# A long-convolution tail on one core: the last half source gets a program and loads of its own

## The chip, the cores and the metric

The kernel runs on one core of a Trainium2 chip. The metric is device time in microseconds (us) for one execution, the lower the better. TensorE (PE) does the matrix products, VectorE (DVE), ScalarE (ACT) and GpSimd (POOL) do elementwise work, and SyncE (SP) issues every DMA transfer of this kernel, strictly in the order of the program. All data are 32-bit floats.

## The reference

Two layers work on an image batch of shape (4, 128, 64, 64), that is 4 sequences of 4096 tokens with 128 channels. Layer 0 (a convolution gate, a sort of patches and a small state-space scan) doesn't matter here. Layer 1 adds two parts to the tokens: a state-space scan over 256 state entries (`_L1_attn_ref`), and a spectral convolution (`_L1_ffn_ref`) of the normalised sum. The second is what the change touches:

```python
Vf = jnp.fft.rfft(phi, n=n, axis=0)
Uf_p = jnp.fft.rfft(u, n=n, axis=1)
Uf_m = jnp.fft.rfft(u * sgn3, n=n, axis=1)          # sgn3: +1, -1, +1, ...
U_plus = jnp.fft.irfft(Vf[None, :, :, None] * Uf_p[:, :, None, :], n=n, axis=1)[:, :sl]
U_minus = jnp.fft.irfft(Vf[None, :, :, None] * Uf_m[:, :, None, :], n=n, axis=1)[:, :sl]
U_minus = U_minus * sgn[None, :, None, None]
...
out = jnp.einsum('btkd,k,kde->bte', U_plus, s, Mpp)
out = out + jnp.einsum('btkd,k,kde->bte', U_minus, s, Mpm)
```

It is a causal convolution of every channel with 16 filters (index k), once plain and once with alternating sign, each followed by a 128 x 128 matrix. A short convolution over three tokens (`_compute_ar_u`) is added, and four branches of decreasing length are mixed with weights. The output at a token depends on all tokens before it, so the last tokens' outputs can only be finished when the scan has ended.

## The kernel before

**Layer 1's main loop.** The program is written out by hand in its final order; no scheduler moves anything. `parts` lists 32 parts, each a chunk of 512 tokens of one sequence; the last one is chunk 7 of sequence 3. A part has 256 steps, one for each state entry. A step scans two rows of 512 tokens on DVE (`scan`, L1236) in place in `ring`, an SBUF tile of five slots; one slot holds four steps (VD = 4). POOL fills a slot (L1220), ACT makes the decay factors (L1232). Every eight steps (GD = 8, two slots) PE contracts the two slots with the matrix c (L1266), in six pieces of which one is taken at each of the following steps. ACT moves the result out of PSUM, a DMA puts it into DRAM (`yd`), and four small DMAs (L1292, "takes") read a skewed view of it back into the tile `yt`.

**The output of a part.** `output` (L979) turns `yt` of a finished part into tokens: it loads x2 (L984) and the gate (L986), transposes yt in two halves of 128 columns (L991), multiplies by the gate (L993), multiplies by W_out (L997), adds x2 (L999), transposes (L1005), normalises, reverses the tokens' order with a flip product (L1016) and copies them into a tile `tok` (L1018). Then it transposes once more (L1022), makes the three-token convolution (L1036) and writes the sum to DRAM as x3 (L1039). It is a generator: inside the loop `beside` runs it piece by piece at steps of the next part. It yields at the points where PE or another engine should take the next bit. PSUM has one bank for all these products (`middle`).

**The spectral program.** Tokens are kept apart by parity (even and odd), so a block of 1024 tokens is a tile of 2 parities x 4 groups of 128 tokens x 128 channels, reversed in time. A task names an output block, the source blocks whose tokens it takes, and whether it ends the block (`full`) or leaves a partial sum in DRAM. `products` (L1096) works tasks off as items, one for each output parity r, filter k and side (the parity of the taps). An item loads a strip of the filter, a window of up to 896 values that slides by one from partition to partition (L1093), and a matrix (L1087), three items ahead and into three strip buffers and four matrix buffers. It multiplies tok by the strip (L1179, the convolution), ACT copies the result out of PSUM (L1191), and a second product with the matrix (L1121) adds it to `fin`. At the end of an r, the partial sum is added by a product with the identity (L1129) and the result to x3 (L1137); after r = 1 a DMA stores the output block (L1139).

**The last block.** Block 3 of sequence 3 is made in stages. Its last stage takes the source's second half, the groups 2 and 3 of 128 tokens of each parity, which are the last part's tokens. It has 2 x 16 x 2 = 64 items; each has convolution products of 256 and 128 columns, an eviction of 256 columns and a second product of 256 columns. It comes after the loop: first the leftover pieces and takes, then the last output with spectral work between its pieces, then `go_on` (L1386) until the spectral program has been idle 16 times.

Of the kernel before, what the change touches and what calls it, by code (L numbers as in the profile page):

```python
# [8 lines left out]
F32 = mybir.dt.float32  # L9
AF = mybir.ActivationFunctionType  # L10
ALU = mybir.AluOpType
# [4 lines left out]
NB = 4  # L16
# [641 lines left out]
TS = 512  # L658
NCH = L // TS
NT = TS // 128  # L660
GD = 8
VD = 4
NQ = 5
NK = 16
# [241 lines left out]
def layer1(ctx: ExitStack, tc, ident, weights, work, psum, second, phi, pqd, mud, x, omd, permd, first, x2, x3, out):  # L906
# [15 lines left out]
    nc = tc.nc  # L922
# [3 lines left out]
    wk = ctx.enter_context(tc.tile_pool(name="s_wk", bufs=2))  # L926
    sp = ctx.enter_context(tc.tile_pool(name="s_sp", bufs=3))
# [3 lines left out]
    pc = ctx.enter_context(tc.tile_pool(name="s_pc", bufs=2, space=PSUM))  # L931
    pf = ctx.enter_context(tc.tile_pool(name="s_pf", bufs=1, space=PSUM))
# [4 lines left out]
    wo, at = weights[3:]  # L937
# [3 lines left out]
        out=flip, in_=flip, compare_op=ALU.not_equal, fill=1.0, base=-127, pattern=[[1, 128]],  # L941
# [35 lines left out]
    tokens = {}  # L977

    def output(b, ch, yt, gate):  # L979


        cols = bass.ts(ch, TS)
        xr = small()
        nc.sync.dma_start(xr, x2[b][:, cols])  # L984
        yk = wide()
        nc.sync.dma_start(yk, gate)  # L986
        for k in range(2):
            yield "mm"
            ps = middle()
            for i in range(NT):  # L990
                nc.tensor.transpose(ps[:, bass.ts(i, 128)], yt[:, i, bass.ts(k, 128)], ident)  # L991
            yield "post"
            nc.vector.tensor_tensor(yk[:, k, :], ps, yk[:, k, :], ALU.mult)  # L993
        yield "mm"
        ps = middle()
        for k in range(2):
            nc.tensor.matmul(ps, wo[:, k, :], yk[:, k, :], start=k == 0, stop=k == 1)  # L997
        yield "post"
        nc.vector.tensor_tensor(xr, xr, ps, ALU.add)  # L999
        yield "mm"  # L1000
        pair = xr.rearrange("p (a q) -> p q a", q=2)
        tp = middle()
        for r in range(2):
            for i in range(2):
                nc.tensor.transpose(tp[:, bass.ts(2 * r + i, 128)], pair[:, r, bass.ts(i, 128)], ident)  # L1005
        yield "post"
        tk = small()
        nc.scalar.copy(tk, tp)
        yield "free"
        yield from normalise(tk.rearrange("p (i c) -> p i c", i=NT))  # L1010
        yield "mm"
        if ch % 2 == 0:
            tokens[b, ch // 2] = sp.tile([128, 2, 4, 128], F32, tag="tok", name="tok", bufs=6)
        tok = tokens[b, ch // 2]
        ps = middle()
        nc.tensor.matmul(ps, flip, tk, start=True, stop=True)  # L1016
        yield "post"
        nc.scalar.copy(tok[:, :, bass.ts(ch % 2, 2), :], ps.rearrange("p (r i c) -> p r i c", r=2, i=2))  # L1018
        yield "mm"
        up = middle()  # L1020
        for i in range(NT):
            nc.tensor.transpose(up[:, bass.ts(i, 128)], tk[:, bass.ts(i, 128)], ident)  # L1022
        mu = small()[:, 0:384].rearrange("p (i c) -> p i c", i=3)
        nc.sync.dma_start(mu, mud[:, (0, 1, 2, 2, 3, 3, 3, 3)[ch]])
        yield "post"
        ut = sm.tile([128, 2 + TS], F32, tag="t2", name="ut", bufs=3)
        nc.scalar.copy(ut[:, 2:].rearrange("p (a q) -> p q a", q=2), up.rearrange("p (q a) -> p q a", q=2))
        if ch:
            nc.scalar.copy(ut[:, 0:2], halos[b % 2])
        else:  # L1030
            nc.scalar.activation(ut[:, 0:2], ident[:, 0:2], AF.Copy, scale=0.0)
        nc.scalar.copy(halos[b % 2], ut[:, TS:])
        yield "mm"
        ps = middle()
        for i in range(3):
            nc.tensor.matmul(ps, mu[:, i, :], ut[:, bass.ds(2 - i, TS)], start=i == 0, stop=i == 2)  # L1036
        yield "post"
        nc.vector.tensor_tensor(xr, xr, ps, ALU.add)
        nc.sync.dma_start(x3[b][:, cols], xr)  # L1039
        if (b, ch) == (NB - 1, NCH - 2):  # L1040
            add([(b, 3, [(3, range(2))], True, False)])
        elif (b, ch) == (NB - 1, NCH - 1):
            add([(b, 3, [(3, range(2, 4))], True, True)])
        elif ch % 2:
            block(b, ch // 2)

    later = []
    queue = []  # L1050
    strips, mats = {}, {}
    row = 128 + L // 2
    now = [0]
    partial = dr.tile([2, 4, 2, 128, TS], F32, name="partial", bufs=1)

    def block(b, blk):

        if b < NB - 2:  # L1060
            tasks = [(b, blk, range(blk + 1), False, True)]
        else:
            tasks = (
                [(b, 0, [0], False, True), (b, 2, [0], False, False), (b, 3, [0], False, False)],
                [(b, 1, [0, 1], False, True), (b, 2, [1], True, False), (b, 3, [1], True, False)],
                [(b, 2, [2], True, True), (b, 3, [2], True, False)],
                [(b, 3, [3], True, True)],
            )[blk]
        add([(b, blk, [(src, range(4)) for src in srcs], *rest) for b, blk, srcs, *rest in tasks])

    def add(tasks):
        for task in tasks:
            queue.extend(
                (task, r, k, side, n)
                for r in range(2) for k in range(NK) for side in range(2) for n in range(len(task[2]))
            )
# [132 lines left out]
    def carry(b, ch, d, ready):  # L1209

        af, vf = ready[4:]
        last = lasts[b % 2]
        cols = bass.ds(d, 128)
        if ch:
            nc.gpsimd.tensor_tensor(af[:, :, cols], af[:, :, cols], last[:, :, cols], ALU.mult)
            nc.gpsimd.tensor_tensor(vf[:, :, cols], vf[:, :, cols], af[:, :, cols], ALU.add)
# [88 lines left out]
    parts = [(b, ch) for b in range(NB - 2) for ch in range(NCH)]  # L1305
    parts += [(b, ch) for ch in range(NCH) for b in (NB - 2, NB - 1)]
    ready = {0: first}
    dls = {}
    ring = wk.tile([128, NQ, VD, 2, TS], F32, name="ring", bufs=1)
    steps = 256 * len(parts)  # L1310
    pieces = []
    side, kind = None, None
    spectral, credit = products(), 0

    def beside(n):

        if n:
            yield from output(*parts[n - 1], done.pop(n - 1), ready.pop(n - 1)[2])
        else:
            yield from put_back()  # L1320
        if n + 1 < len(parts):
            ready[n + 1] = tiles(n + 1)
            yield from project(*parts[n + 1], ready[n + 1])

    done, takes = {}, []
# [9 lines left out]

    for k in range(-12, steps):
        now[0] = k
        j = k + 10
        if 0 <= j < steps and j % 128 == 0:
            carry(*parts[j // 256], j % 256, ready[j // 256])  # L1340
        j = k + 6
        if 0 <= j < steps and j % VD == 0:
            spread(j // VD, j % 256, dls[j // VD], ready[j // 256])
        j = k + 1
        if 0 <= j < steps:
            lift(j % 256, factors[j % 2], dls[j // VD])
        j = k + 10
        if 0 <= j < steps and j % VD == 0:
            dls[j // VD] = fetch(j % 256, ready[j // 256])
        j = k + 2  # L1350
        if 0 <= j < steps and j % VD == 0:
            begin(j // VD, j % 256, ready[j // 256])
        if k < 0:
            continue
        due()
        n, d = divmod(k, 256)
        b, ch = parts[n]
        if pieces:
            pieces.pop(0)()
        scan(k, factors[k % 2])  # L1360
        if d % GD == GD - 1:
            more, take = contract((k - GD + 1) // VD, ready[n][1], d // GD, lasts[b % 2] if ch + 1 < NCH else None)
            pieces += more
            takes.append((n, take))
        if d == GD:
            side = beside(n)
            kind = next(side, None)
        at_step = d % GD
        if kind == "free" or (kind == "mm" and at_step == 6) or (kind == "post" and at_step == 7):
            kind = next(side, None)  # L1370
        if at_step == GD - 1:
            fetch_y(n, d)
        pace = 1.4 if n < 2 * NCH else 1.7
        credit = min(credit + pace * TS, pace * TS)
        while credit > 0:
            cost = next(spectral)
            if cost == 0:
                break
            credit -= cost
    for piece in pieces:  # L1380
        piece()
    while takes:
        fetch_y(len(parts), 0)
    idle = 0

    def go_on():  # L1386
        nonlocal idle
        now[0] += 1
        due()
        idle = 0 if next(spectral) else idle + 1  # L1390

    for _ in beside(len(parts)):
        go_on()
        go_on()
    idle = 0
    while idle < 16:
        go_on()


@with_exitstack  # L1400
# [72 lines left out]
```

## Time and profile before

| | |
|---|---|
| Median of 3 runs | 21174.41 us (21171.87 to 21175.32) |
| The profiled execution, its own time | 21175.71 us |
| Its span in the profile | 21174.0 us |
| Busy: PE, DVE, ACT, POOL | 17593.0, 20421.0, 15775.4, 19750.3 us |
| Mean granted PE clock | 0.917 |
| Last scan step ends | 21000.9 us |
| Tokens of the last part copied (L1018 starts) | 21032.32 us |
| First product of the last stage starts | 21045.46 us |
| Last add on DVE, and last store issued | 21169.58 and 21170.30 us |

Times in the tail count from the start of the span. The busy shares are of the whole span, of which the part after the last scan step is 173 us. A float product shows as two records in the profile, so "x4" are two products. A line number names the line of the kernel that issued an instruction, and "DMA a<-b" is a transfer's time until landing.

### The profile page before, as it was taken

The numbers are of one execution on the slowest core, as the hardware profiler recorded it, in microseconds if no ns is written. First come the engines' busy times: TensorE is split into PE (matmuls) and PEld (weight loads), VectorE is DVE, ScalarE is ACT, GpSimd is POOL, SyncE is SP. The second block draws the span as 40 slices with busy tenths as digits, with TensorE's granted clock in tenths as the row PEclk, the third lists the DMA queues.
The fourth block names the chain that finished last, engine by engine and source line by source line (L and its number), as shares of the span: only waits on it lengthen the run. The fifth ranks groups of instructions, "written<-read, shape, count | busy, mean of one in ns | idle before, by whom it ended". The sixth has DMA issues, their size and how long they took to land.

```text
span 21174.0 us, 282862 instructions
## 1 busy us (share of the span) xinstructions
PE 17593.0 (83%) x99308; PEld 7771.7 (37%) x99308; DVE 20421.0 (96%) x11805; ACT 15775.4 (75%) x28243; POOL 19750.3 (93%) x3541
## 2 busy tenths in 40 slices
PE   7788844655858888877768999599999999999997
PEld 4344421322323333333323344243434434344434
DVE  7799999999999999999999999999999999999996
ACT  3667667777777777777777777788887787788875
POOL 2666699999999999999999999999999999999996
PEclk8999966777979999988979999699999999999999
DMA  1555544555656666666656777577777777777776
GB/s 68 133 143 144 144 163 155 185 172 174 220 176 221 223 226 224 223 208 199 205 192 221 231 240 238 174 237 234 239 236 231 235 234 235 237 234 233 232 224 187
DMA packets 2204928, 4303.20 MB, mean 203 GB/s; under 512 B 770633, under 2 KB 1290097, under 8 KB 1938161
## 3 DMA queue, kind: packets, MB, share of 16 engines
q1 hardware_dynamic: 2203504, 4285.10, 63.0%
q8 instruction: 786, 12.88, 0.2%
q14 instruction: 638, 5.22, 0.1%
HBM read 3660.02 MB, written 624.17 MB: 202 GB/s over the span
## 4 chain that ended last, share of the span: by engine, by line
DVE 53%; issue 15%; PE 11%; ACT 4%; POOL 3%; DMA 1%; SPq 0%; DVEq 0%; POOLq 0%; ACTq 0%
DVE ring L1236 52%; PE conv L1179 6%; POOL ring L1220 3%; PE yp L1266 3%; ACT da L1232 2%; PE fin L1121 1%; DMA strip<-in_phi 1%; ACT conved L1191 1%; PE mm L1036 0%; PE mm L883 0%; PE mm L877 0%; PE mm L868 0%; ACT t L804 0%; ACT ye L1273 0%; DVE st L789 0%
## 5 line engine op out<-in xcount | busy, mean ns | idle before, releaser
L1220 POOL TENSOR_TENSOR ring<-u,dlb 128x4088 f32<-128x4088 f32 x2048 | 18074.9, 8892 | 70.5 <-DMA dlb<-delta 42.1
L1236 DVE TENSOR_TENSOR_SCAN ring<-da,ring 128x1024 f32<-128x1024 f32 x8192 | 17927.9, 2266 | 182.4 <-ACT da L1232 154.0
L1232 ACT ACTIVATE da<-dlb,at 128x511 f32<-128x511 f32 x16384 | 11321.1, 691 | 4052.2 <-DVE ring L1236 3766.3
L1179 PE MATMUL conv<-strip,tok 128*128 128x512 f32 (+3 forms) x20480 | 8632.2, 549 | 83.0 <-DMA strip<-in_phi 82.0
L1266 PE MATMUL yp<-ring,c 128*32 128x256 f32 x65536 | 4931.5, 430 | 2482.1 <-DVE ring L1236 1284.9
L1179 PEld LDWEIGHTS conv<-strip,tok 128*128 128x128 f32 x20480 | 3652.7, 191 | 4172.4 <-issue 3732.6
L1266 PEld LDWEIGHTS yp<-ring,c 128*32 128x32 f32 x65536 | 2011.7, 119 | 6185.4 <-issue 3454.8
L532 POOL TENSOR_TENSOR v<-dx,bcb 128x1024 f32<-128x1024 f32 x512 | 1208.6, 2361 | 631.7 <-DVE states L554 627.5
L1121 PE MATMUL fin<-conved,pq 128*128 128x512 f32 (+1 forms) x3968 | 1789.0, 543 | 9.1 <-ACT sum L1142 4.8
L546 ACT ACTIVATE f<-dt,an 128x255 f32<-128x255 f32 x2048 | 974.7, 476 | 490.9 <-DVE states L554 440.2
L554 DVE TENSOR_TENSOR_SCAN states<-f,v 128x1024 f32<-128x1024 f32 x512 | 1176.0, 2297 | 106.1 <-ACT f L546 54.5
L1273 ACT COPY ye<-yp 128x512 f32<-128x512 f32 x2048 | 1185.9, 579 | 24.1 <-PE yp L1266 23.1
L1191 ACT COPY conved<-conv 128x512 f32<-128x512 f32 (+1 forms) x1728 | 986.7, 571 | 255.4 <-PE conv L1179 252.4
L570 PE MATMUL y<-p,ident 128*128 128x512 f32 x2048 | 1010.4, 619 | 173.7 <-DVE p L558 170.1
L1121 PEld LDWEIGHTS fin<-conved,pq 128*128 128x128 f32 x3968 | 664.8, 192 | 387.1 <-issue 279.1
L558 DVE TENSOR_TENSOR p<-states,bcb 128x1024 f32<-128x1024 f32 x512 | 627.0, 1225 | 38.3 <-DVE states L554 0.4
L570 PEld LDWEIGHTS y<-p,ident 128*128 128x128 f32 x2048 | 364.6, 194 | 710.0 <-issue 336.6
L1226 ACT COPY ring<-vf 128x8 f32<-128x8 f32 x2048 | 386.8, 189 | 4.1 <-DMA omd<-om 4.1
L462 PE MATMUL mm<-ow,yg 128*32 128x128 f32 x2048 | 250.8, 276 | 39.0 <-ACT om L466 37.7
L462 PEld LDWEIGHTS mm<-ow,yg 128*32 128x32 f32 x2048 | 219.3, 133 | 136.2 <-ACT om L466 60.8
L1279 ACT COPY last<-ring 128x8 f32<-128x8 f32 x1792 | 267.0, 198 | 0.0
L407 PE MATMUL mm<-xin,taps 128*128 128x512 f32 x512 | 236.3, 605 | 22.8 <-ACT an L378 19.9
(229 smaller groups left out, 5356.2 us busy)
## 6 DMA issues: line engine op xcount, KB each, us to landing
dlb<-delta SPq DMA_DIRECT2D x2048, 1024.0 KB, 5.3
strip<-in_phi SPq DMA_DIRECT2D x1536, 448.0 KB, 5.0
yd<-ye SPq DMA_DIRECT2D x2048, 256.0 KB, 4.6
strip<-in_phi SPq DMA_DIRECT2D x1088, 256.0 KB, 4.8
bcb<-bcd SPq DMA_DIRECT2D x1024, 256.0 KB, 4.2
pq<-pqd SPq DMA_DIRECT2D x1472, 64.0 KB, 4.2
yt<-yd SPq DMA_DIRECT2D x4096, 4.0 KB, 4.4
pq<-pqd SPq DMA_DIRECT2D x256, 128.0 KB, 4.2
```

The source lines that it names most:

```text
L532: nc.gpsimd.tensor_tensor(v, ready[n][2][:, :, bass.ts(i, SUB)].unsqueeze(1).broadcast_to((128, 2, 2, SUB)), bc[:, 0].unsqueeze(2).broadca ...
L546: nc.scalar.activation(factors[j % 2][:, a, k, 1:], ready[n][1][:, k, SUB * i + 1 : SUB * i + SUB], AF.Exp, scale=an[:, k, 2 * g + a : 2 * ...
L554: nc.vector.tensor_tensor_scan(states.rearrange(flat), factors[j % 2].rearrange(flat), v.rearrange(flat), 0.0, ALU.mult, ALU.add)
L570: nc.tensor.matmul(t.rearrange("p k t -> p (k t)"), ident, p[:, a].rearrange("p k t -> p (k t)"), start=g == 0 and a == 0, stop=False, ski ...
L1121: nc.tensor.matmul(fin[:, bass.ds(c0, w)], pq[:, n, :], u[:, bass.ds(c0, w)], start=begin and n == 0, stop=end and not partly, skip_group_ ...
L1179: nc.tensor.matmul(ps[:, skip:], tok[:, 1 - r if side else r, j, :], strip[:, bass.ds(c0 - lo, TS - skip)], start=which == 0 and j == js[0 ...
L1191: nc.scalar.copy(u[:, cols], ps[:, cols])
L1220: nc.gpsimd.tensor_tensor(ring[:, q % NQ, :, :, 1:], ready[0][:, :, 1:].unsqueeze(1).broadcast_to((128, VD, 2, TS - 1)), dl[:, :, 1:].unsq ...
L1232: nc.scalar.activation(da[:, h, 1:], dl[:, d % VD, 1:], AF.Exp, scale=at[:, h, d : d + 1])
L1236: nc.vector.tensor_tensor_scan(v, da.rearrange("p h t -> p (h t)"), v, 0.0, ALU.mult, ALU.add)
L1266: nc.tensor.matmul(yp[i // 2][bass.ts(p, 32), i % 2], c[:, h, t], moving(h, 128 * i + 32 * p, 32), start=h == 0, stop=h == 1,)
L1273: nc.scalar.copy(ye, yp[j].rearrange("p i d t -> p i t d"))
```

## The change

The last stage no longer goes through `products`. A generator of its own, `last_products`, computes it for both output parities at once: for each filter k and token parity p it multiplies tok by a window with 256 columns for each of the two output parities, side by side in one PSUM bank (512 columns for group 2, twice 128 for group 3). ACT evicts p = 0, DVE p = 1. Two products of 512 columns with the two matrices of the filter then add both parities to one `fin`, a filter later.

All matrices of the stage (2 MB) are loaded into one slot of the ring ten steps before the loop ends. The filter windows of 7 + 7 filters go into two more slots and those of the last two into strip tiles, in eight transfers, after the takes. The two partial sums and the first half of x3's block are loaded right behind them. The partial sums are added to x3's tile by DVE, while the products run, and x3's last chunk stays in SBUF. The block's output is stored in two halves.

The first piece of the last output (its loads of x2 and of the gate) is taken before the leftover pieces and takes. Since the tile of y is then looked up before the last takes fill it, it is no longer popped from the table, so that those takes still go to that tile. The spectral program is run dry before the last output goes on, and the products of the last stage start as soon as the output has yielded "tokens".

```diff
@@ output @@
         nc.scalar.copy(tok[:, :, bass.ts(ch % 2, 2), :], ps.rearrange("p (r i c) -> p r i c", r=2, i=2))
+        final = (b, ch) == (NB - 1, NCH - 1)
+        if final:
+            yield "tokens"
...
         nc.vector.tensor_tensor(xr, xr, ps, ALU.add)
+        if final:
+            closing.append(xr)
+            return
         nc.sync.dma_start(x3[b][:, cols], xr)
         if (b, ch) == (NB - 1, NCH - 2):
             add([(b, 3, [(3, range(2))], True, False)])
-        elif (b, ch) == (NB - 1, NCH - 1):
-            add([(b, 3, [(3, range(2, 4))], True, True)])
+    closing = []
+    WS = 256 + 257
+    MS = VD * 2 * TS // WS
+    def slot(n):
+        return ring[:, (steps // VD + n) % NQ].rearrange("p d h t -> p (d h t)")
+    def matrices_of_last():
+        pq = slot(-5).rearrange("p (k s c) -> p k s c", k=NK, s=2)
+        for side in range(2):
+            nc.sync.dma_start(pq[:, :, side], pqd[:, side, :, 3].rearrange("k c e -> c k e"))
+        return pq
+    def strips_of_last():
+        at = []
+        k = 0
+        for room in (
+            slot(-4)[:, 0 : MS * WS], slot(-3)[:, 0 : MS * WS],
+            *(sp.tile([128, 896], F32, tag="strip", name="strip")[:, 0:WS] for _ in range(NK - 2 * MS)),
+        ):
+            room = room.rearrange("p (k t) -> p k t", t=WS)
+            n = room.shape[1]
+            for side in range(2):
+                start = (NK * side + k) * row + 1 - side
+                nc.sync.dma_start(
+                    room[:, :, 256 * side : WS - 257 * (1 - side)],
+                    bass.AP(phi.tensor, start, [[1, 128], [row, n], [1, 256 + side]]),
+                )
+            at += [room[:, i] for i in range(n)]
+            k += n
+        return at
+    def last_products(pq, strips):
+        b, blk = NB - 1, 3
+        tok = tokens[b, 3]
+        fin = pf.tile([128, TS], F32, tag="fin", name="fin")
+        def raw(t, offset, dims):
+            return bass.AP(t.tensor, t.offset + offset, [list(t.ap[0]), *dims])
+        def add_up(k, u):
+            nc.tensor.matmul(fin, pq[:, k, 0], raw(u, 0, [[TS, 2], [1, 256]]), start=k == 0, stop=False)
+            nc.tensor.matmul(
+                fin, pq[:, k, 1], raw(u, TS + 256, [[-TS, 2], [1, 256]]), start=False, stop=k == NK - 1
+            )
+        before = None
+        for k in range(NK):
+            u = wk.tile([128, VD, TS], F32, tag="dlb", name="u", bufs=3)[:, 0:2].rearrange("p a t -> p (a t)")
+            for p in range(2):
+                ps = pc.tile([128, TS], F32, tag="conv", name="conv")
+                to = ps.rearrange("p (s t) -> p s t", s=2)
+                for j in (2, 3):
+                    skip = 128 * (j - 2)
+                    nc.tensor.matmul(
+                        to[:, :, skip:], tok[:, p, j, :],
+                        raw(strips[k], 0, [[256 + 1 - p, 2], [1, 256 - skip]]), start=j == 2, stop=j == 3,
+                    )
+                if p:
+                    nc.vector.tensor_copy(u[:, TS:], ps)
+                else:
+                    nc.scalar.copy(u[:, 0:TS], ps)
+            if before:
+                add_up(*before)
+            before = k, u
+            yield
+        add_up(*before)
+        yield fin
@@ beside @@
-            yield from output(*parts[n - 1], done.pop(n - 1), ready.pop(n - 1)[2])
+            yield from output(*parts[n - 1], done[n - 1], ready.pop(n - 1)[2])
@@ the loop @@
         now[0] = k
+        if k == steps - 10:
+            matrices_ = matrices_of_last()
@@ after the loop @@
+    rest = beside(len(parts))
+    next(rest)
     for piece in pieces:
         piece()
...
-    for _ in beside(len(parts)):
-        go_on()
-        go_on()
-    idle = 0
     while idle < 16:
         go_on()
+    strips_ = strips_of_last()
+    parted = []
+    for r in range(2):
+        parted.append(sp.tile([128, TS], F32, tag="conved", name="sofar"))
+        nc.sync.dma_start(parted[r], partial[(NB - 1) % 2, 3, r])
+    x6 = sp.tile([128, 2 * TS], F32, tag="xo", name="xo", bufs=1)[:, 0:TS]
+    nc.sync.dma_start(x6, x3[NB - 1][:, bass.ts(NCH - 2, TS)])
+    while next(rest) != "tokens":
+        pass
+    spectral = last_products(matrices_, strips_)
+    for _ in rest:
+        next(spectral)
+    next(spectral)
+    xr = closing.pop()
+    for half, t in enumerate((x6, xr)):
+        for r in range(2):
+            dst = t.rearrange("p (a q) -> p q a", q=2)[:, r, :]
+            nc.vector.tensor_tensor(dst, dst, parted[r][:, bass.ts(half, 256)], ALU.add)
+        if half == 0:
+            nc.sync.dma_start(out[NB - 1][:, bass.ts(NCH - 2, TS)], t)
+    for fin in spectral:
+        pass
+    dst = xr.rearrange("p (a q) -> p q a", q=2)
+    nc.vector.tensor_tensor(dst, dst, fin.rearrange("p (q a) -> p q a", q=2), ALU.add)
+    nc.sync.dma_start(out[NB - 1][:, bass.ts(NCH - 1, TS)], xr)
```

## The prediction

> **What bounds the kernel now.** I read the chain of waits over the last 300 us first, then the PE groups by shape in the tail, the busy time by stage, and last the order of the PE instructions inside the loop. The page's part 4 places the bulk, 52% of the whole span: the scan on DVE.
>
> ```profile
> DVE ring L1236 52%; PE conv L1179 6%; POOL ring L1220 3%; PE yp L1266 3%; ACT da L1232 2%; PE fin L1121 1%; DMA strip<-in_phi 1%; ACT conved L1191 1%; PE mm L1036 0%; PE mm L883 0%; PE mm L877 0%; PE mm L868 0%; ACT t L804 0%; ACT ye L1273 0%; DVE st L789 0%
> ```
>
> The diff doesn't touch that loop: up to the last ten scan steps the changed program has the same instructions in the same order on every engine. All can only happen after about 20979 us, and mostly after the last scan ends at 21001. So the tail is what is priced. Its chain of waits (start, length, what):
>
> ```profile
> 21012.69 4.21 DMA t<-gate
> 21017.00 0.70 DVE t L993
> ...
> 21032.32 0.59 ACT tok L1018
> ...
> 21059.18 3.40 DMA strip<-in_phi
> 21062.58 0.14 issue
> 21062.71 0.89 PE conv L1179 x4
> 21063.60 0.45 PE fin L1121 x2
> ...
> 21169.58 0.69 DVE xo L1137
> ```
>
> Two stretches: 21001 to 21041, the output of the last part, one short step after another; then 21041 to 21174, a cycle of load, products, load. The cycle takes about 5.3 us, mostly for three items: a strip is loaded only when its buffer, one of three, is free, and the load from 21059.18 is late for the product at 21062.71. The PE groups by shape in that stretch say the same: PE waits 37.6 us for strips, while its columns are few.
>
> ```profile
> L1179 PE MATMUL conv<-strip,tok 128*128 128x256 f32 x128 | 44.5, 430 | 38.2 <-DMA strip<-in_phi 37.6
> L1121 PE MATMUL fin<-conved,pq 128*128 128x256 f32 x128 | 39.3, 390 | 0.3 <-issue 0.2
> ```
>
> What PE needs without waits is read inside the loop, where it is saturated (PE by time):
>
> ```profile
> 20906.66 2.32 PE L1179 MATMUL conv<-strip,tok 128*128 128x512 f32 x8
> 20908.82 1.02 PE L1121 MATMUL fin<-conved,pq 128*128 128x512 f32 x2
> 20909.68 1.67 PE L1179 MATMUL conv<-strip,tok 128*128 128x512 f32 x4
> ```
>
> Start to start, 512+384+256+128 columns take 2.16 us and 512 take 0.86: 1.69 ns a column. The clock by 5 us windows:
>
> ```profile
> 21045.00:21050.00 5.00, 2.92 (x8) 2.27 (x9) 0.00 (x0) 0.37 (x1) 0.00 (x0) 0.50 0.81 185
> 21050.00:21055.00 5.00, 4.87 (x16) 3.74 (x15) 0.00 (x0) 1.12 (x3) 0.00 (x0) 0.59 0.65 196
> 21055.00:21060.00 5.00, 3.75 (x18) 2.70 (x18) 0.00 (x0) 0.87 (x3) 0.00 (x0) 1.00 0.75 173
> ```
>
> Third column from the right: half clock first, full about 21054, some 5 to 8 us after work resumed.
>
> **What the Trainium skill says.** "TensorE: Matmul & The Clock Gate", Part 1: the array runs at half rate until a window of about 3.4 us has been busy. The trace agrees in kind, 5 us or more here. "DMA: Bandwidth & Descriptors", Anatomy of one DMA: about 2 us of each transfer is fixed. The trace: 1.6 us for the 4 KB yt reads, 3.6 us for a 256 KB strip; a scheme of 64 short-lived strips pays this again and again. Same page, Latency and other measured facts: a row pitch of 512 KiB gave 207 GB/s. The matrix load below steps 512 KiB from filter to filter in DRAM; no run here shows such a load.
>
> **The change, part by part.**
>
> 1. *The gate and x2 loads (L984, L986) go ahead of the leftover pieces.* Before, they stand on SP's queue behind the last yt reads, and DVE L993 starts at 21017.00 on the gate. After, they are issued at about 21000.2, behind the yt reads of 20998.38, and land by 21005 (4.2 us). The first L993 then follows its transposes (end 21009.1) at 21009.4. What is late next is the second set of transposes, which needs all of yt: the last yt read issues at 21011.75 and lands 1.65 later, 21013.4, against 21017.74 before. Gain 4.3 us, kept along the serial chain: tokens ready (end of L1018) 21032.9 - 4.3 = 21028.6. Keeping the y tile in the table instead of popping it changes no instruction in the loop; it is needed only because the tile is taken early.
>
> 2. *Matrices, two 1 MB loads at ten steps before the end.* SP reaches them after the put at about 20978.8, ahead of four yt reads, and they wait for PE's products on that ring slot (ended 20976). No delta fetch comes after them, so the scan cannot wait on them. Behind them on SP: the yt reads of 20981, and those of 20998.4, which reuse the same completion slots and so wait for landing. 2 MB at 207 GB/s is an estimate of 10 us plus 2: landed by 20992. Cost nothing, under cover of the scan. The cover is gone if they land after about 21002 (under 95 GB/s), when the put of 21005.3 would be late, us for us.
>
> 3. *Strips.* The first issues where L984 stood, 21012.2, after all yt reads, so those aren't held up. Of each ring slot's two loads the second waits for the first to land, as the changed program orders them. Each is 7 x 128 runs of 1 KB, 0.92 MB. Nearest row: 1024 KB of dlb in 5.3 us, with 2 KB runs. I take 6 us: first pair landed by 21025, second by 21035. Upper bound: at the tail's 181 GB/s, 1.84 MB take 10.1 us plus twice 2, so 21027; if the third load shares the engines with the second, 21030. Needed 21028.6 for filter 0; filters 7 to 13 at about 21060. Cost 0, at most 2 us. The mu load, queued behind them, partial sums and x, lands by about 21040, needed after filter 2's first products, about 21043.
>
> 4. *The 64 items become 16 filters.* Per filter: two tokens' parities x (512+256) columns plus two products of 512, 2560 columns; 16 x 2560 = 40960, as before (64 x 640). At 1.69 ns: 69.2 us. Into it fall the last output's mu products, 3 x 512 columns, 2.6 us, and four transposes, 0.5 us. Half clock for the first 5 to 6 us loses 2.7. The two evictions per filter are hidden: ACT about 0.6 us and DVE 0.7 us against 4.3 us of PE per filter, with two PSUM banks and the previous filter's products between. Removed: the cycle's waits, the two identity products of the partial sum, 2 x 0.86, and the 4.5 us wait for a partial sum at 21104.7. The partial adds move to DVE, four of 256 columns, about 0.4 each (half of 0.69), during filters 5 on, when DVE has some 3.6 us free per filter. The x load's wait also falls there.
>
>    Unknown: products read in two separate runs of 256 or 128 columns. Lower bound, no extra. Upper: L1266, whose operand lies in eight runs of 32, takes 1.00 us for 16 records, that is 8 x 256 columns in four column groups, against 0.86 by column count: 16%, or 11 us. I take nothing, since runs here are 4 to 8 times longer; both ends go into the range.
>
> 5. *The end.* One DVE add, 0.69, and a 256 KB store in place of 512 KB. Store before: issue at 21170.30, 2.6 us to landing, end 1.1 later. I take 2.1 + 1.1.
>
> Sum: 21028.6 + 69.2 + 2.6 + 0.5 + 2.7 = 21103.6; release 0.3, add 0.7, store 3.2: **21107.8** against the span's 21174.0, so -66. The profiled execution took 21175.71, span plus 1.7; the median shown is 21174.41. Applied to the median: **21108 us**, -0.31%. A measurement here can tell about 0.2%, 42 us.
>
> **Rivals.**
>
> *The loads stay the wait.* The serial pairs of strips, or the matrices, land late. Place: the first product of filter 0. Every us past 21028.6 costs one. For: 1 KB and 512 B runs, and a false order between the two loads of a slot. Against: 4 us of margin, and nothing else in flight. Some 3 to 15 us lost: 21111 to 21123. Still faster.
>
> *PE stays at half clock, or the edit brings nothing.* Then 72 us become 144: 21108 + 70 = about 21178, no change. For: in the stretch 21001 to 21041 the clock is mostly 0.50. Against: whenever PE is dense it runs at 1.00, from 20800 to 20900 for instance, and even with the tail's gaps.
>
> *Slower: split operands.* If a product whose moving operand is in separate runs cost several times its columns, 69 us would grow; it decides for slower beyond 66 + 42 = 108 us more, a factor of 2.6 (4.3 ns a column). At a factor of 3, 138 us more: 21246. Against: L1266's 16% with far shorter runs. A step from one run back to an earlier one, which a fifth of the columns have (8192, 13.8 us), is shown by nothing in this trace; alone it would need a factor of about 9.
>
> **How the numbers follow.** Forecast with its bounds 0.83 (its own range 21101 to 21115), late loads 0.10, half clock or nothing gained 0.05, split operands 0.02. Below the forecast lie a clock already warm at the tokens (2 to 3 us) and the earlier transposes running at full clock (2); above it the 11 us of short runs and late loads. Range 21100 to 21123. Faster by over 0.2% takes the first two cases, 0.93; within 0.2% the third, 0.05; slower 0.02.
>
> **What would show it.** Step 1: the first L993 no longer waits for the gate, and the second transposes wait for yt. Step 2: scans at 2.18 us to the end and no gap at the put of 21005. Step 3: the first conv product released by the tok copy and not by a strip. Step 4: PE busy without gaps, 4.3 us from filter to filter, clock 1.00 after the first two. Step 5: the end some 4 us after the last product. Wrong if the first product is released by a DMA, if filters take 5 us or more, or if the clock stays under 1.00.

## The result and the profile after

The changed kernel takes 21106.47 us (median of 7 runs, 21105.12 to 21110.48) beside 21175.32 us for the kernel before on the same chips. The ratio is 0.9967, with a 95% interval of 0.9956 to 0.9979. That is some 69 us less at the medians, and all of it lies after the last scan.

The span is 21105.0 us. The chain of waits of the kernel after, over its tail (start, length, what), where L1344 is the old L1266 and L1370 the old L1292:

```profile
21010.70 1.73 DMA yt<-yd
21012.43 0.09 issue
21012.52 1.10 PE mm L991 x4
...
21024.56 2.09 PE mm L1016 x2
21026.65 0.02 issue
21026.68 0.59 ACT tok L1018
21027.27 0.04 issue
21027.31 4.62 PE conv L1111 x8
21031.94 0.44 PE mm L1025 x4
21032.37 2.58 PE conv L1111 x8
21034.96 0.86 PE fin L1098 x2
21035.81 0.86 PE fin L1099 x2
...
21100.28 0.87 PE fin L1099 x2
21101.15 0.02 issue
21101.17 0.69 DVE t L1499
```

The transfers that filled more than half of the old chain after 21041 are gone. In the kernel before, the shares of that chain were:

```profile
by line: DMA strip<-in_phi 54.8%; PE conv L1179 16.5%; PE fin L1121 8.9%; DMA sofar<-partial 5.3%; SPq L1087 5.2%; issue 3.3%; PE fin L1129 1.7%; SPq L1093 0.7%; DVE t L1038 0.5%; DVE xo L1137 0.5%; SPq L1039 0.2%; SPq L1127 0.0%
```

Now the last transfer on the chain is the last yt read; after it come the short steps of the output, then the copy of the tokens releases the first product, and from there PE goes on without a break until the last add. A filter takes 2.58 + 0.86 + 0.86 = 4.30 us, 15 times alike. The groups of the tail by shape (busy and mean, then idle time and its releaser) say who waits now:

```profile
L1111 PE MATMUL conv<-ring,tok 128*128 128x512 f32 x56 | 30.1, 620 | 0.7 <-ACT tok L1018 0.7
...
L1116 DVE COPY u<-conv 128x512 f32<-128x512 f32 x16 | 11.1, 692 | 64.4 <-PE conv L1111 50.5 <-DMA strip<-in_phi 10.9 <-ACT u L1118 3.0
L1118 ACT COPY u<-conv 128x512 f32<-128x512 f32 x16 | 9.4, 586 | 59.6 <-PE conv L1111 59.6
```

PE's products wait 0.7 us in all; the two evicting engines wait for PE. The 10.9 us that DVE's line puts down to a strip's transfer is idle time before DVE's first eviction (21031.97), which starts as soon as PE's first eight records have ended (21031.93). The clock in windows of 5 us (third column from the right) is at half when the products begin and full from about 21031 on:

```profile
21025.00:21030.00 5.00, 4.33 (x6) 1.57 (x6) 0.00 (x0) 0.59 (x1) 0.00 (x0) 0.50 0.56 129
21030.00:21035.00 5.00, 5.00 (x18) 3.02 (x17) 0.70 (x2) 1.85 (x5) 0.00 (x0) 0.91 0.89 236
21035.00:21040.00 5.00, 5.00 (x15) 2.50 (x14) 1.38 (x2) 0.70 (x2) 0.00 (x0) 1.00 0.33 125
```

SP's queue by time shows the loads: matrices under the last scans, L984 and L986 ahead of the last puts, the strips behind the yt reads.

```profile
20978.93 2.11 SPq L1065 DMA_DIRECT2D ring<-pqd  x2
20981.15 5.22 SPq L1370 DMA_DIRECT2D yt<-yd  x4
...
20999.83 0.43 SPq L984 DMA_DIRECT2D t<-x  x1
21000.31 0.43 SPq L986 DMA_DIRECT2D t<-gate  x1
21004.70 2.96 SPq L1352 DMA_DIRECT2D yd<-ye  x2
21009.39 1.74 SPq L1370 DMA_DIRECT2D yt<-yd  x4
21011.24 14.93 SPq L1080 DMA_DIRECT2D ring<-in_phi  x4
```

### The profile page after: what moved, and what is told of

Its sections match the earlier page's. It is cut to its first block, busy times and chain, and to the rows that moved or that the text cites. A ratio compares the mean times of both kernels' runs of the same rounds, so it can differ in the third digit from the quotient of the medians.

```text
span 21105.0 us, 282109 instructions
## 1 busy us (share of the span) xinstructions
PE 17551.7 (83%) x99112; PEld 7740.7 (37%) x99112; DVE 20433.2 (97%) x11824; ACT 15761.0 (75%) x28195; POOL 19751.2 (94%) x3541
## 4 chain that ended last, share of the span: by engine, by line
DVE 51%; issue 15%; PE 12%; POOL 5%; ACT 4%; DMA 1%; DVEq 0%; SPq 0%; POOLq 0%; ACTq 0%
DVE ring L1314 49%; PE conv L1257 6%; POOL ring L1298 4%; PE yp L1344 3%; ACT da L1310 2%; PE fin L1199 1%; ACT conved L1269 1%; DMA strip<-in_phi 0%; ACT t L804 0%; PE mm L883 0%; PE mm L877 0%; PE mm L868 0%; PE mm L1039 0%; PE conv L1111 0%; ACT ye L1351 0%
## 5 line engine op out<-in xcount | busy, mean ns | idle before, releaser
L1344 PE MATMUL yp<-ring,c 128*32 128x256 f32 x65536 | 4917.1, 428 | 2493.9 <-DVE ring L1314 1283.8
L1257 PEld LDWEIGHTS conv<-strip,tok 128*128 128x128 f32 x20224 | 3606.1, 191 | 4105.8 <-issue 3722.3
L1344 PEld LDWEIGHTS yp<-ring,c 128*32 128x32 f32 x65536 | 2007.5, 119 | 6188.5 <-issue 3468.9
L1269 ACT COPY conved<-conv 128x512 f32<-128x512 f32 x1664 | 963.0, 579 | 146.3 <-PE conv L1257 143.2
```

What stands on the lines that cost most here:

```text
L1257: nc.tensor.matmul(ps[:, skip:], tok[:, 1 - r if side else r, j, :], strip[:, bass.ds(c0 - lo, TS - skip)], start=which == 0 and j == js[0 ...
L1269: nc.scalar.copy(u[:, cols], ps[:, cols])
L1344: nc.tensor.matmul(yp[i // 2][bass.ts(p, 32), i % 2], c[:, h, t], moving(h, 128 * i + 32 * p, 32), start=h == 0, stop=h == 1,)
```

## The experiments

The last scan ends between 20993.0 and 21001.4 us in the profiles below, although the program up to there is the same (apart from the place of the matrix load, and the unread products of e6_warm and e8_best). So the tails are compared from the end of the last scan: to the end of the tokens' copy (L1018), and from there to the end of the last DVE add. Each number is a difference of two times in that kernel's profile.

| kernel | scan end to tokens | tokens to last add | tail |
|---|---|---|---|
| before | 32.0 | 137.4 | 169.4 |
| e1_gate: early x2 and gate alone | 27.6 | 135.4 | 163.0 |
| e2_narrow: half the strip bytes | 31.5 | 128.4 | 159.9 |
| after | 26.8 | 74.6 | 101.4 |
| e3_shape: bulk loads, old products | 29.1 | 75.9 | 105.0 |
| e4_three: small loads, new products | 29.7 | 75.7 | 105.4 |
| e5_late: bulk loads after the tokens | 26.8 | 89.8 | 116.6 |
| e6_warm: clock held up, first try | 26.6 | 74.2 | 100.8 |
| e7_mlate: matrices ahead of the strips | 29.1 | 78.2 | 107.4 |
| e8_best: clock held up, loads rearranged | 23.0 | 72.8 | 95.8 |

**e1_gate.** One part of the change alone:

```diff
-            yield from output(*parts[n - 1], done.pop(n - 1), ready.pop(n - 1)[2])
+            yield from output(*parts[n - 1], done[n - 1], ready.pop(n - 1)[2])
...
+    rest = beside(len(parts))
+    next(rest)
     for piece in pieces:
         piece()
...
-    for _ in beside(len(parts)):
+    go_on()
+    go_on()
+    for _ in rest:
         go_on()
         go_on()
```

> The kernel before with one part of the change: x2 and the gate of the last output are loaded ahead of the leftover pieces and takes, and the y tile stays in its table. My theory: from the end of the last scan to the finished tokens 27 to 29 us instead of 32.05, the first gate product no longer waits for the gate, and the rest of the tail stays at 137 us. Rival: the tokens come earlier but the loads of the last stage do not, so the tail after them grows by what is gained.

A single run took 21164.6 us. The tokens come 27.6 us after the scan, 4.4 earlier than before (some 0.4 of it because PE's short bursts on the way found a higher clock), and the rest of the tail isn't longer (135.4). The rival falls. The old chain's wait for the gate is replaced by that for yt, as in the changed kernel.

**e2_narrow.** Half the bytes:

```diff
-        width = 896 if src < blk else 512
+        width = 896 if src < blk else 256 if sources[which][1][0] == 2 else 512
```

> The kernel before, but the strips of the last stage are loaded 256 columns wide, which is all that its products read, instead of 512: half the bytes, the same 64 items, three buffers and order. My theory: the cycle of the old tail (5.3 us for three items) is made of a fixed time per load and the hand-over between PE, SP and the buffer, so halving the bytes shortens each landing from 3.6 us to about 2.8 and the tail by 12 to 20 us of its 124. Rival: the tail was bound by bytes; then the 37.6 us of waiting for strips go almost wholly, 30 us or more.

Measured: ratio 0.9998 (0.9989 to 1.0006), no change that the times can tell; in the profile, 9 us less between tokens and end. That is less than the 12 to 20 us expected, and far from the rival's 30. The landing (least, median, most) of the strips, first in the old kernel's tail and then in this one's:

```profile
DMA to landing us min/median/max: 3.3/3.6/5.8
```

```profile
DMA to landing us min/median/max: 3.0/3.3/4.8
```

Half the bytes take 0.3 us off a landing, even less than the 0.8 that I expected. Over some 21 cycles of three items that makes 6 to 7 of the 9 us. PE still waits 30.6 us for strips, against 37.6. The old tail was not bound by bytes in the main.

**e3_shape.** The changed kernel's loads with the old products:

```diff
+        for r in range(2):
+            for k in range(NK):
+                for side in range(2):
+                    u = wk.tile([128, VD, TS], F32, tag="dlb", name="u", bufs=3)[:, 0, 0:256]
+                    ps = pc.tile([128, TS], F32, tag="conv", name="conv")
+                    for j in (2, 3):
+                        skip = 128 * (j - 2)
+                        nc.tensor.matmul(
+                            ps[:, skip:256], tok[:, 1 - r if side else r, j, :],
+                            strips[k][:, bass.ds((256 + r) * side, 256 - skip)], start=j == 2, stop=j == 3,
+                        )
+                    nc.scalar.copy(u, ps[:, 0:256])
...
```

> The changed kernel with all its early bulk loads, but the last stage's products in the old shape: 64 items, one for each output parity, filter and side, with products of 256 and 128 columns, an eviction of 256 columns on ACT alone and a second product of 256. The columns are the same, 40960. My theory: columns at 1.69 ns set the time and the shape does not, so the span is that of the changed kernel within 2 us (21105). Rival: the merged, wider products are a part of the gain, because weight loads of 190 ns no longer hide behind records of 64 to 128 columns or because evictions interrupt PE; then items take 1.3 us instead of 1.08 and the span is 14 us longer.

Measured: ratio 0.9970 (0.9959 to 0.9982), median 21109.26 us. After the tokens it takes 75.9 us, 1.3 more than the changed kernel. Its chain of waits in the middle of the stage:

```profile
21042.03 0.65 PE conv L1118 x4
21042.68 0.43 PE fin L1106 x2
21043.12 0.65 PE conv L1118 x4
21043.77 0.43 PE fin L1106 x2
```

An item takes 1.09 us from start to start, four of them 4.35 against 4.30 for a filter of the new shape. So the merged products are not where the gain comes from, once the loads are there. The 2.3 us that this run loses ahead of the tokens are the clock's (last section): its last contraction took 3.64 us instead of 1.93.

**e4_three.** The changed kernel's products with three strip buffers:

```diff
+    def load_of_last(k):
+        strip = sp.tile([128, 896], F32, tag="strip", name="strip")[:, 0:WS]
+        pq = sp.tile([128, 2, 128], F32, tag="pq", name="pq", bufs=4)
...
             before = k, u
+            if k + 3 < NK:
+                loaded.append(load_of_last(k + 3))
             yield
...
-    strips_ = strips_of_last()
+    loaded_ = [load_of_last(k) for k in range(3)]
```

> The changed kernel's products, but no load into the ring: each filter's two windows go into one of three strip buffers and its two matrices into one of four small buffers, loaded three filters ahead, the first three as early as the changed kernel's strips. My theory: a buffer now stands for 4.3 us of products instead of 1.08, so three of them cover 3.6 to 7 us of landing, PE never waits, and the span is that of the changed kernel within 3 us (21105). Rival: loading everything at once is what gains; then every filter waits for its small loads, 2 us or more each, and the span is 30 us or more longer.

Measured: ratio 0.9969 (0.9956 to 0.9981), median 21107.69 us. PE doesn't wait for a load in the stage:

```profile
L1096 PE MATMUL conv<-strip,tok 128*128 128x512 f32 x64 | 34.6, 624 | 0.7 <-ACT tok L1018 0.7
```

Both halves of the change, the bulk loads and the wider work for each buffer, remove the old wait by themselves; together they add nothing that these profiles can tell. Three buffers that stood for 3 x 1.08 us of products couldn't cover a landing of 3.6 us with its hand-over; three that stand for 3 x 4.30 do. One thing isn't separated here: since a window now serves both output parities, e3_shape and e4_three also load 4 MB of strips where the old stage loaded 16, in 8 and 32 transfers instead of 64. e2_narrow says what half the bytes alone are worth; no run gives the old loads more buffers and nothing else.

**e5_late.** A small transfer of the tokens ahead of the strips on SP's queue:

```diff
+    while next(rest) != "tokens":
+        pass
+    nc.sync.dma_start(dr.tile([128, 4], F32, name="mark", bufs=1), tokens[NB - 1, 3][:, 0, 3, 0:4])
     strips_ = strips_of_last()
...
-    while next(rest) != "tokens":
-        pass
```

> The changed kernel, but a 2 KB transfer of a corner of the finished tokens stands on SP's queue ahead of the strips, so that all strips, partial sums and x are loaded only after the tokens exist. The second load of the first pair then lands about 14 to 15 us after the tokens. My theory: the first product waits for it and everything behind shifts by 14 to 15 us, to a span of about 21120, still 54 us under before: the early start is worth a quarter of the gain. Rival: the later loads also fall behind PE (third and fourth load, or the small matrices of the three-token convolution), and the loss is 20 us or more.

Measured: ratio 0.9974 (0.9965 to 0.9984), a median of 21118.28 us and a span of 21120.4 us. The chain of waits, and PE's wait in the stage:

```profile
21027.26 0.34 SPq L1478
...
21027.71 6.89 DMA ring<-in_phi
...
21035.09 8.18 DMA ring<-in_phi
21043.28 0.02 issue
21043.29 6.47 DMA ring<-in_phi
21049.77 0.02 issue
21049.78 6.00 DMA t<-mud
```

```profile
L1111 PE MATMUL conv<-ring,tok 128*128 128x512 f32 x56 | 30.1, 621 | 14.3 <-DMA ring<-in_phi 14.3
```

The products' wait grows from 0.7 to 14.3 us, now for the loads, and the three-token convolution waits 1.3 us for its small matrices: together 14.9 of the 15.2 us that the stage after the tokens is longer. So these bulk loads need their early start; without it they give back 15 us. That is no share of the 68 us gained over the kernel before, whose small loads also started late and held up its first product by 5.1 us.

**e6_warm.** Unread products in PE's idle stretches:

```diff
+    def warm(n):
+        ps = pc.tile([128, TS], F32, tag="conv", name="warm")
+        for _ in range(n):
+            nc.tensor.matmul(ps, ident, weights[0], start=True, stop=True)
     rest = beside(len(parts))
     next(rest)
+    warm(5)
...
+    next(rest)
+    warm(4)
+    for _ in range(7):
+        next(rest)
+    warm(5)
```

> The changed kernel with 14 more products of identity and a weight tile into a free PSUM bank, whose results nothing reads, put into PE's idle stretches of the tail: 5 before the last contraction, 4 after the first transposes of yt, 5 before the flip. My theory: they only hold the granted clock at full rate, so that the last contraction takes 2 us instead of 3.4, the W_out products 1.7 instead of 3.4, the flip 0.9 instead of 2.1 and the first convolution products 2.6 instead of 4.6: about 7 us from the last scan's end to the end, 94 us instead of 101.4. Rival: they stand in the way on PE's queue, or the clock doesn't follow them, and the tail is not shorter.

Measured: median 21100.64 us, but a tail of 100.8 us, not 94. PE by time (the view begins at 20988, so its first line has only five of the ten records of the first five products):

```profile
20987.73 2.31 PE L1463 MATMUL warm<-win,ident 128*128 128x512 f32 x5
20993.18 3.64 PE L1344 MATMUL yp<-ring,c 128*32 128x256 f32 x32 [3.14 <-DVE ring L1314]
20997.52 3.64 PE L1344 MATMUL yp<-ring,c 128*32 128x256 f32 x32 [0.69 <-ACT ye L1351]
...
21009.08 1.98 PE L997 MATMUL mm<-t,wo 128*128 128x512 f32 x4 [0.78 <-DVE t L993]
...
21017.85 1.12 PE L1016 MATMUL mm<-t,flip 128*128 128x512 f32 x2 [0.96 <-ACT t L804]
21019.65 2.85 PE L1111 MATMUL conv<-ring,tok 128*128 128x512 f32 x8 [0.68 <-ACT tok L1018]
```

The first five ended 3.1 us ahead of the last contraction, and both contractions ran at half clock. From L997 on the clock followed as expected (1.98, 1.12 and 2.85 us). So the mechanism holds and its first placing failed. What it gained was given back: the two contractions took 2.0 us longer than in the changed kernel, the second transposes now stood behind the unread products, and the three-token convolution waited 1.1 us for its small matrices. Since the contractions' speed differs by chance too, this run alone doesn't size it.

**e7_mlate.** The matrices loaded without the scans' cover:

```diff
-        if k == steps - 10:
-            matrices_ = matrices_of_last()
...
+    matrices_ = matrices_of_last()
     strips_ = strips_of_last()
```

> The changed kernel with the 2 MB of matrices loaded after the takes, directly ahead of the strips, instead of under the last scans. My theory: the strips then queue behind them; the first pair lands 5 to 6 us later, 3 to 4 us after the tokens, and the tail is 3 to 5 us longer than the changed kernel's. Rival: the cover is worth more, because the small matrices of the three-token convolution also fall behind, 8 us or more; or the margin of the strips hides it and nothing changes.

A single run, 21114.05 us. The products wait 2.4 us for the strips:

```profile
L1111 PE MATMUL conv<-ring,tok 128*128 128x512 f32 x56 | 30.5, 628 | 2.4 <-DMA ring<-in_phi 2.4
```

In the changed kernel they wait 0.7, for the tokens. The small matrices cost another 0.6, and the stage after the tokens takes 78.2 us, 3.6 more; 0.8 of that are slower first products (5.46 us against 4.62). The cover is worth what was expected. The tail's other 2.4 us lie ahead of the tokens and are PE's clock, as in e3_shape: the last contraction took 3.64 us instead of 1.93, the W_out products 3.78 instead of 3.40.

**e8_best.** The same unread products, placed anew (7, 4 and 5), the small matrices ahead of the strips, and the two window sets of a slot apart from each other:

```diff
+    warm(7)
     for piece in pieces:
...
+    early.append(slot(-4)[:, MS * WS : MS * WS + 384].rearrange("p (i c) -> p i c", i=3))
+    nc.sync.dma_start(early[0], mud[:, 3])
     strips_ = strips_of_last()
...
                 nc.sync.dma_start(
-                    room[:, :, 256 * side : WS - 257 * (1 - side)],
+                    room[:, bass.ds(256 * n * side, (256 + side) * n)].rearrange("p (k t) -> p k t", k=n),
                     bass.AP(phi.tensor, start, [[1, 128], [row, n], [1, 256 + side]]),
                 )
...
-                        raw(strips[k], 0, [[256 + 1 - p, 2], [1, 256 - skip]]), start=j == 2, stop=j == 3,
+                        raw(strips[k][0], 0, [[strips[k][1] + 1 - p, 2], [1, 256 - skip]]), start=j == 2, stop=j == 3,
```

> The changed kernel with 7 + 4 + 5 unread products that keep PE's clock up (7 ahead of the last contraction instead of 5, which ended 3 us too early in the last run), the small matrices of the three-token convolution loaded ahead of the strips into the spare end of a ring slot, and the two window sets of a slot in separate stretches, so that the second load no longer waits for the first. My theory: the last two contractions take 2 us each, the W_out products 2, the flip 1.1, the first convolution products 2.7, and no load is waited for: tokens 22 us after the last scan instead of 26.8, the end 73 us after the tokens, a tail of 95 us instead of 101.4, and a median some 5 us under the changed kernel. Rival: the early products again end too early or hold up the chain on PE's queue, and the tail stays at 100 to 101 us.

Measured: median 21098.18 us (21093.88 to 21098.53), ratio 0.9965 (0.9951 to 0.9979). PE by time:

```profile
20984.51 7.41 PE L1466 MATMUL warm<-win,ident 128*128 128x512 f32 x14
20993.27 1.93 PE L1347 MATMUL yp<-ring,c 128*32 128x256 f32 x32 [1.35 <-DVE ring L1317]
20995.90 1.93 PE L1347 MATMUL yp<-ring,c 128*32 128x256 f32 x32 [0.69 <-ACT ye L1354]
```

The contractions take 1.93 us each, the tokens come 23.0 us after the scan and the tail is 95.8 us, 5.6 less than the changed kernel's; expected were 95. The median lies 8.3 us under that of the changed kernel, from other runs, and the intervals of the two ratios overlap: by the times alone the two can't be told apart. The tails, of one profile each, differ by 5.6 us; that is more than the 2.3 us that the clock cost e3_shape ahead of the tokens, and the changed kernel's own profile had the lucky clock. The median of e8_best is the lowest here.

## Why the prediction was right

Forecast were 21108 us and a span of 21107.8; measured were 21106.47 and 21105.0. The 2.8 us between the spans, step by step:

1. *Gate and x2.* Right: the second transposes start at 21012.52, released by the last yt read, and the tokens are finished 26.75 us after the last scan; 27.7 were forecast from before's times. The remaining microsecond is luck, a clock that happened to be up earlier: the two contractions took 3.37 and 1.93 us (3.64 and 2.37 before) and the W_out products 3.40 (3.78). In e3_shape, with the same work up to there, the tokens took 29.1. e1_gate shows the step alone: 4.4 us, about 4.0 without the clock's part, against 4.3 forecast.
2. *Matrices.* Right. The first landed 6.3 us after its issue. The trace has no landing of the second, but the busy share of the DMA engines is 0.73 from 20985 to 20990 and 0.14 in the next 5 us, so both were over by about 20990; 20992 was estimated. That is well ahead of the yt reads of 20998. It doesn't test the rate that the prediction took from the Trainium skill ("DMA: Bandwidth & Descriptors", Latency and other measured facts): the pitch there lies between partitions, and here the 512 KiB lie between the filters' pieces of one partition. The last scan ended at 21000.5, before at 21000.9. e7_mlate puts the cover at some 4 us after the tokens.
3. *Strips.* Right at the points used: nothing waited for them. Landings of 5.8 to 8.2 us stand against the 6 assumed, and the second load of each pair waited for the first, as forecast. The fixed 2 us in the bounds are the figure of the Trainium skill ("DMA: Bandwidth & Descriptors", Anatomy of one DMA) for transfers that GpSimd issues; here SP issues them, and the 4 KB yt reads landed 1.5 to 1.8 us after issue when no large load was under way. e5_late shows that the early start was needed.
4. *Products.* Right, and split operands cost nothing: 2560 columns in 4.30 us are 1.68 ns a column, against 1.69 forecast, or 0.4 us over all. The mis-sized term is the half clock: the first eight records took 4.62 us against 2.58 later, a loss of 2.04 and not 2.7. One reading is off without touching the sum: the partial sum's load of 4.5 us, named among the waits removed, kept PE waiting for 1.4 us only.
5. *The end.* From the last add's end to the span's end 3.1 us, 3.2 forecast; the release of the add took 0.02 us instead of 0.3.

The rivals fell by the trace: no product was released by a strip, the clock was 1.00 once PE had been busy for about 4 us, and an operand in two runs is as fast as one in a single run, the backward step included.

What the prediction left open is whether "all at once" was needed. The experiments say that it wasn't: the old wait fits a queue too shallow in time. It goes with all loads ahead, or with more work for each buffer, both with fewer bytes and transfers.

## What to carry to other kernels

Count a prefetch queue in microseconds of the consumer's work, not in buffers: three buffers of 1.08 us starve behind a landing of 3.6 us, three of 4.30 us don't. Halving the bytes took only 9 of 137 us off this loop's stage. When a stage can only start late, look for the loads whose data do not depend on what it waits for, and put them on the queue ahead of it; the bulk loads here cost 15 us when they started after the tokens. Compare short tails from a common event inside the profile when run-to-run differences ahead of it are as large as the effect.

## What the runs showed of the hardware that was not expected

- The speed of one and the same short burst depends on when it falls, and not only on PE's work before it: the contraction of 32 records took 1.93 to 3.64 us, the W_out products 1.98 to 3.78 us, with the granted clock between 0.50 and 1.00. The tokens' time after the scan differed by 2.3 us between the changed kernel and e3_shape (26.8 and 29.1 us), which are equal up to there.
- The traces show where this comes from. In the tail of every one of them the granted clock changes only at instants that are whole multiples of 3.41 us apart, and these instants fall differently in each run. In the changed kernel four of them are near 20990.0, 20993.4, 20996.8 and 21003.6 us; the clock's rise at the last lies between its last two contractions (21000.7 and 21004.7), so the second ran at full clock. In e3_shape no rise came between 20990.6 and 21014.5, and both ran at half. How busy PE must be between two such instants is not shown.
- In e6_warm the clock was full while the first unread products ran; it fell at about 20992.1, 2.1 us after their end and 1.1 us before the contraction. With a gap of 1.35 us it stayed up (e8_best).
- Two loads of 0.9 MB one after the other landed 5.8 and 6.2 us after their issue (the changed kernel); four issued together landed after 6.0 to 14.1 us each (e8_best). But all four were there 15.8 us after the first issue, and 21.7 us after it in the changed kernel.
